# Half of the adjacency factors made on VectorE in the first group of heads, with two side queues that start late

## The chip, the cores and the metric

The kernel runs on one core of one Trainium2 chip. The metric is the device time in microseconds of one launch, taken as the median of several runs.

## The reference, cut to what matters

Two layers of a graph network are computed for 3327 nodes with 128 features, over one adjacency matrix `adj` of zeros and ones. The first layer is a graph attention layer, the second has 128 attention heads of width 8 (d is the number of heads here, h the width).

```python
# layer 0
H = X @ W.T + b
e = leaky_relu(A * (H @ a_s) + A * (H @ a_r).T, 0.2)
att = softmax(where(A > 0, e, NEG), axis=1)
x = layernorm(x + att @ H)
# layer 1: q, k, v are (d, n, h) with d = 128 heads of width h = 8
a = einsum('dnh,dmh->dnm', q, k) * d ** -0.5
a = softmax(a + adj + adj, axis=2)          # both encodings are adj
out = einsum('dnm,dmh->dnh', a, v).reshape(n, h * d)
x = layernorm(x + out @ Wo.T)
```

The second layer costs nearly all of the time: 128 heads with a score matrix of 3327 x 3327 each.

## The kernel before, in words

**Groups, blocks, rounds.** The heads are taken in NG = 32 groups of HG = 4. A group takes the queries in NBLK = 7 blocks of 476 (the last has 472). A block goes over NT = 26 tiles of up to 128 keys in NR = 26 rounds, so a group has `total` = 182 rounds. In each round, TensorE makes two halves of scores (two heads of one key tile each, 128 x 952), and TensorE multiplies an earlier key tile's weights by the values, LAG = 5 rounds behind (line 957). The exponential is exp(2(s + adj)), since scores are scaled by one half of the usual factor.

**Two ways to put adj in.** Key tiles are taken in threes (a *stretch*, three rounds; a block has nine stretches or, in the other order, ten). Two tiles of a three are *added*: VectorE writes scores + adj (line 1177), and ScalarE takes the exponential of all four heads at once (line 1000, 128 x 1904). The third is *multiplied*: ScalarE takes the exponential of the bare scores (line 1174, 128 x 952), and GpSimd multiplies it by a factor, 1 where adj is 0 and e squared where it is 1 (line 1175). So a block has 17 or 18 multiplications on GpSimd and 34 or 35 additions on VectorE.

**The factors.** Each block of queries has nine factor tiles of 128 x 476. They are made once, in the first group of heads, by `make_factor` (line 794): one multiply-and-add in place, at the end of the stretch ahead of the one that uses it. Two rounds later SyncE stores it to device memory (`ftd`), from where every later group loads it. That makes 63 factors, all in group 0. Loads of adj are issued AHEAD = 3 stretches in advance from SyncE's queue (`want_adj`).

**The side work.** Layer 0 for row tile 0 is done before the groups begin. Row tiles 1 to 25 of layer 0, with their projections to q, k and v, and the final projection of each tile (`result`) are spread between the rounds. `work` and `work_tensor` take units from three queues, in this order: `main` (products, normalization, projections, results), `aside` (weights of a tile: `weigh` line 308 and `mask` line 317, both on GpSimd, kind "m") and `counts` (`count`, line 326 on VectorE, kind "d"; it counts zeros and ones of adj for a check, and after each six counts the queue loads a part of the next tile's adj). `lane` gives one place for a "d" unit and one for an "m" unit about every third round, 7 of each in a block; the first queue that has a unit of the kind at its head takes the place. A unit "n" at the head of a queue waits for a mark, "t" sets one, "w" waits some rounds. A tile is worked on in three chunks of 9, 9 and 8 key tiles.

**Due times.** `finish_to` at round 164 of a group runs at once whatever the next group still needs: tile 1 for group 1, tile 2 for group 2, and so on.

The order on each engine is fixed when the program is built. The few lines that set the places:

```python
n -= odd
if n == NR - 2 and odd:
    return int(kind != "l")
if kind == "l" and n == -1:
    return 1
if n < 6:
    return int(kind == "l" and n == 0 and not odd)
return int(n % 3 == {"q": 0, "l": 2}.get(kind, 1) or n % 3 == 1 and kind == "q")
```

Of the kernel before, what the change touches and what calls it, by code (L numbers as in the profile page):

```python
# [13 lines left out]
ALU = mybir.AluOpType  # L14
# [13 lines left out]
E2 = 7.38905609893065  # L28
# [19 lines left out]
def kernel(  # L48
# [27 lines left out]
    nc = tc.nc  # L76
# [73 lines left out]
    def special():  # L150
# [9 lines left out]
        with ExitStack() as sx, tc.manual_schedule(engines=ALL):  # L160
# [94 lines left out]
            def issue(f):  # L255
                pend.append([ISSUE, f])
# [485 lines left out]
            def kind(g, b):  # L742

                return (g * NBLK + b) % 2
# [41 lines left out]
            def make_factor(n):  # L786
                if n < len(stretches):
                    g, b, m = stretches[n]
                    times, _ = plans[kind(g, b)][m]
                    if times is None or made_by[b, times] != n:  # L790
                        return
                    w = exact[b][2]
                    f = adjs[n][:, 0, :w]
                    nc.gpsimd.tensor_scalar(f, f, E2 - 1.0, 1.0, op0=ALU.mult, op1=ALU.add)  # L794
                    issue(lambda: nc.sync.dma_start(ftd[b][times // 3][:, :w], f))


# [209 lines left out]
            total = NBLK * NR  # L1007
# [19 lines left out]
            made = [layer0(t) for t in range(1, NT)]  # L1027
            first_loads = made[0][0]
            main = []
            aside, counts = [], []  # L1030
            for n, (_, m, a) in enumerate(made):

                k = 0
                for u in a:
                    if u[0] == "r":

                        at = max((k for k, v in enumerate(aside) if v[0] == "n" and v[1][0] == "P"), default=0)
                        aside.insert(at, ("x", u[1]))
                    elif isinstance(u, list):
                        counts += u  # L1040
                        if n + 1 < len(made):
                            counts += [("n", ("W", (n + 1) * len(CH) + k, 0)), made[n + 1][0][k], ("t", ("L", (n + 2) * len(CH) + k))]
                        k += 1
                    else:
                        aside.append(u)
                main.append(m)
# [8 lines left out]
            def head(row, now, force=False):  # L1055

                while True:
                    if not side[row]:
                        if row != "main":
                            return None  # L1060
                        ahead = ("rows", reads[min(max(now, 0) // total + 2, NG - 1)]) in marks
                        if results and results[0][0] <= now and (ahead or not main):
                            side[row] = results.pop(0)[1]
                        elif main:
                            side[row] = main.pop(0)
                        else:
                            return None
                    kind, f = side[row][0]
                    if kind == "t":
                        marks[f] = now  # L1070
                    elif kind == "w":
                        if not force and now - side["since"][row] < f:
                            return None
                    elif kind == "n":
                        if f[:2] not in marks or not force and now - marks[f[:2]] < f[2]:
                            return None
                    else:
                        return kind
                    side[row].pop(0)
# [5 lines left out]
            def work_tensor(now, n, odd):  # L1085

                kind = head("main", now)
                if kind in ("p", "q") and lane(kind, n, odd) and side["read"] != now - 1:
                    run("main", now)

            def work(now, n, odd):
                room, low, pool = lane("d", n, odd), lane("l", n, odd), lane("m", n, odd)
                for row in ("main", "aside", "counts"):
                    while True:
                        kind = head(row, now)
                        if kind == "x":
                            pass
                        elif kind == "d" and room:
                            room -= 1
                            if row == "main":  # L1100
                                side["read"] = now
                        elif kind == "l" and low:
                            low -= 1
                            side["read"] = now
                        elif kind == "m" and pool:
                            pool -= 1
                        else:
                            break
                        run(row, now)

            def finish_to(mark, now):
                while mark not in marks:
                    at = -1 if now is None else now
                    row = next((row for row in ("main", "aside", "counts") if head(row, at, True)), None)
                    if row is None:
                        break
                    run(row, -1)
                    tick(True)
# [9 lines left out]
            for _, u in first_loads:  # L1128
                u()
            nc.sync.dma_start(wo, woT)  # L1130
            make_factor(0)
            for g in range(NG):
                k4, v4, _ = group
                for b in range(NBLK):
# [5 lines left out]
                    for n, rnd in enumerate(rounds):  # L1140
                        at = b * NR + n
                        if n in starts:
                            m = number[g, b, starts[n]]
                            want_adj(m + AHEAD)
                            a = adjs[m]
# [33 lines left out]
                        now = g * total + at  # L1179
# [4 lines left out]
                        if n + 1 in starts or n + 1 == NR:  # L1184
                            del adjs[m]
                            make_factor(m + 1)
# [139 lines left out]
    def general():  # L1326
        with ExitStack() as gx:
# [168 lines left out]
            with ExitStack() as pc:  # L1496
                wp = pc.enter_context(tc.tile_pool(name="pc_w", bufs=3))
                ps = pc.enter_context(tc.tile_pool(name="pc_ps", bufs=4, space=bass.MemoryType.PSUM))
                for t in range(NT):
# [30 lines left out]
                    nc.scalar.dma_start(out[t * P : t * P + r, :], y[:r])  # L1530

    special()
    fine = nc.values_load(flag[0:1, 0:1])
    with tc.If(fine < 1):
# [41 lines left out]
```

## Time and profile before

| what | us |
|---|---|
| median of 3 runs (lowest to highest) | 9987.08 (9984.36 to 9990.81) |
| the profiled execution's own time | 9985.2 |
| its span, first to last instruction | 9983.4 |
| ScalarE busy in it | 9866.4 (99%) |
| TensorE, VectorE, GpSimd busy | 9441.9, 9189.1, 9175.6 |
| a block of queries at about 645 us | 44.0 |
| a block of queries at about 150 us | 51.7 |

Block times are read from the timeline of VectorE: line 967 copies the finished block once (124.30, 175.98, 227.56, 278.74, 329.34, 373.98, 423.47, 467.14, 512.83 us and so on), so the distance of two copies is one block. Group 0 holds the first seven copies.

### The profile page before, as it was taken

To read this page: it belongs to the slowest core of one execution; us is meant where nothing else is said; L and a number is where in the kernel's file an instruction comes from. 1 tells how busy PE (TensorE), PEld (TensorE's weight loads), DVE (VectorE), ACT (ScalarE), POOL (GpSimd) and SP (SyncE) were. 2 spreads that over 40 slices of the span, in tenths; PEclk is the share of its full clock that TensorE was granted. 3 is DMA by queue.
4 is the path that set the end of the run, shared out by engine and by line. 5 is a ranking of instruction groups with operands and counts; after the bars stand their busy time and mean duration, and the time that the engine had idled before them with its cause. 6 is when DMAs were issued, how large, how long until landed. Compare 5 with 4: busy or idle time off the path is not lost.

```text
span 9983.4 us, 207568 instructions
## 1 busy us (share of the span) xinstructions
PE 9441.9 (95%) x79523; PEld 2997.2 (30%) x79523; DVE 9189.1 (92%) x10554; ACT 9866.4 (99%) x7904; POOL 9175.6 (92%) x4954
## 2 busy tenths in 40 slices
PE   7999999999999999999999999999999999999998
PEld 2233233333332333323333233233333322222222
DVE  7899999999999999999999999999999998888888
ACT  7999999999999999999999999999999999999999
POOL 7999899999999999999999999999999988888887
PEclk8999999999999999999999999999999999999999
DMA  6666665666656566565566665666665655555554
GB/s 195 201 185 182 176 185 170 180 182 178 183 172 185 164 182 191 169 187 172 169 183 183 188 175 171 180 180 176 186 169 176 176 164 166 163 158 168 165 166 133
DMA packets 1399415, 1755.28 MB, mean 176 GB/s; under 512 B 349361, under 2 KB 1386891, under 8 KB 1394313
## 3 DMA queue, kind: packets, MB, share of 16 engines
q1 hardware_dynamic: 1388061, 1739.30, 60.5%
q8 instruction: 626, 10.26, 0.4%
q10 hardware_dynamic: 10347, 2.61, 0.1%
q14 instruction: 381, 3.11, 0.1%
HBM read 1637.49 MB, written 103.93 MB: 174 GB/s over the span
## 4 chain that ended last, share of the span: by engine, by line
ACT 43%; PE 30%; issue 10%; POOL 10%; DVE 5%; DMA 1%; SPq 0%; POOLq 0%; DVEq 0%; ACTq 0%
ACT e L1000 31%; PE av L957 15%; PE scb L152 12%; ACT e L1174 12%; POOL e L1175 9%; DVE e L1177 4%; PE bank L241 2%; DVE o L967 1%; DMA at<-in_adjT_dram 1%; POOL w L308 0%; POOL w L317 0%; POOL at L794 0%; DVE lo L409 0%; DMA at<-ftd 0%; DVE dump L326 0%
## 5 line engine op out<-in xcount | busy, mean ns | idle before, releaser
L1175 POOL TENSOR_TENSOR e<-e,at 128x952 f32<-128x952 f32 (+1 forms) x3920 | 8715.4, 2238 | 720.0 <-ACT e L1174 673.0
L1177 DVE TENSOR_TENSOR e<-scb,at 128x952 f32<-128x952 f32 (+1 forms) x7728 | 8501.1, 1142 | 724.3 <-PE scb L152 518.9
L1000 ACT ACTIVATE e<-e 128x1904 f32<-128x1904 f32 (+3 forms) x3920 | 7488.3, 1910 | 10.4 <-DVE e L1177 8.8
L957 PE MATMUL av<-e,v4b 128*32 128x476 f32 (+1 forms) x46592 | 5815.9, 573 | 77.8 <-DVE o L967 36.8
L1174 ACT ACTIVATE e<-scb 128x952 f32<-128x952 f32 (+1 forms) x3920 | 4314.7, 1101 | 53.3 <-PE scb L152 25.2
L152 PE MATMUL scb<-q4b,k4b 32*128 32x476 f32 (+1 forms) x23296 | 3854.1, 485 | 430.1 <-ACT e L1174 302.3
L152 PEld LDWEIGHTS scb<-q4b,k4b 32*128 32x128 f32 (+1 forms) x23296 | 1746.4, 189 | 5403.3 <-ACT e L1174 3189.4
L957 PEld LDWEIGHTS av<-e,v4b 128*32 128x32 f32 (+1 forms) x46592 | 1030.0, 108 | 1244.3 <-issue 1011.5
L241 PE MATMUL bank<-hsb,w 128*32 128x129 f32 (+1 forms) x5200 | 278.3, 286 | 0.0
L326 DVE TENSOR_SCALAR_CACHE_REDUCE dump<-a 128x384 bf16<-128x384 f32 (+2 forms) x468 | 247.3, 528 | 0.6
L308 POOL TENSOR_SCALAR w<-trow,er 128x129 f32<-128x129 f32 x650 | 233.2, 383 | 1.9
L317 POOL TENSOR_TENSOR w<-w,a 128x384 f32<-128x384 f32 (+3 forms) x225 | 209.5, 931 | 0.1
L967 DVE COPY o<-av 128x476 f32<-128x476 f32 (+1 forms) x224 | 144.1, 643 | 7.4 <-PE av L957 7.3
L241 PEld LDWEIGHTS bank<-hsb,w 128*32 128x32 f32 (+1 forms) x5200 | 102.5, 108 | 148.1 <-issue 148.1
L241 PE MATMUL bank<-wo,ot 128*32 128x128 f32 x1600 | 85.2, 285 | 0.0
L402 DVE TENSOR_SCALAR hi<-bank 128x256 fp32r<-128x256 f32 (+1 forms) x200 | 82.8, 414 | 0.0
L409 DVE SCALAR_TENSOR_TENSOR lo<-bank,hi 128x256 fp32r<-128x256 f32 (+1 forms) x200 | 82.8, 414 | 0.0
L241 PE MATMUL bank<-wk,x1T 128*32 128x256 f32 x800 | 63.9, 391 | 0.0
L241 PE MATMUL bank<-wq,x1T 128*32 128x256 f32 x800 | 63.9, 391 | 0.0
L241 PE MATMUL bank<-wv,x1T 128*32 128x256 f32 x800 | 63.9, 391 | 0.0
L503 PE MATMUL bank<-ident,o 128*128 128x128 f32 x225 | 52.0, 304 | 0.0
L290 POOL MEMSET a<- 128x128 f32 (+1 forms) x25 | 5.2, 208 | 45.8 <-DVE dump L326 44.9
(123 smaller groups left out, 653.2 us busy)
## 6 DMA issues: line engine op xcount, KB each, us to landing
at<-in_adjT_dram SPq DMA_DIRECT2D x1536, 476.0 KB
at<-ftd SPq DMA_DIRECT2D x1674, 238.0 KB
at<-in_adjT_dram SPq DMA_DIRECT2D x256, 472.0 KB
at<-ftd SPq DMA_DIRECT2D x279, 236.0 KB
k4b<-kT SPq DMA_DIRECT2D x128, 415.9 KB
q4b<-qT SPq DMA_DIRECT2D x1528, 29.8 KB
at<-in_adjT_dram SPq DMA_DIRECT2D x192, 208.2 KB
at<-in_adjT_dram SPq DMA_DIRECT2D x150, 238.0 KB
```

The costliest lines, as they stand in the source:

```text
L152: nc.tensor.matmul(dst, k4[32 * j : 32 * j + H4, first_key(i) : first_key(i) + 2 * r - 1 : 2], q4[32 * j : 32 * j + H4, :nb], start=True, ...
L241: nc.tensor.matmul(dst[c0:c1], w[:, c0:c1], mov, **kw)
L308: nc.gpsimd.tensor_scalar(w, s["t"][:, :, :T3], -LOWEST, e, op0=ALU.min, op1=ALU.max)
L317: nc.gpsimd.tensor_tensor(w, w, s["a"][n][:, c0 - i0 : c1 - i0, :r], op=ALU.mult)
L326: nc.vector.tensor_scalar(z, a, float(k), None, op0=ALU.is_equal, op1=ALU.add, accum_out=even[:, t, at : at + 1])
L402: nc.vector.tensor_scalar(hi[:r, o : o + QW], s["b"][:r, :QW], scale, None, op0=ALU.mult)
L957: nc.tensor.matmul(s.av[32 * j : 32 * j + 32, : s.w], s.v4[:r, j, i * H1 : i * H1 + 32], e[:r, j, : s.w], start=(s.left == NT - 1), stop=( ...
L967: nc.vector.tensor_copy(o4[:, :w], s.av[:, :w])
L1000: nc.scalar.activation(e, e, AF.Exp, scale=2.0)
L1174: nc.scalar.activation(eh, z[:r, :, :w], AF.Exp, scale=2.0)
L1175: nc.gpsimd.tensor_tensor(eh, eh, ah, op=ALU.mult)
L1177: nc.vector.tensor_tensor(eh, z[:r, :, :w], ah, op=ALU.add)
```

## The change

1. `make_factor` takes VectorE for the stretches of odd number in a block and keeps GpSimd for the others. With nine factors in a block, VectorE gets four in blocks 0, 2, 4 and 6 of group 0 and five in blocks 1, 3 and 5: 31 of 63.
2. A new kind of unit, "a", holds its queue until a given round. The queue `counts` begins with one for round `total * 3 // 5` = 109.
3. The queue `aside` gets one for round `total * 4 // 5` = 145 ahead of the weights of row tile 2 (the second tile of this queue).

```diff
-                    nc.gpsimd.tensor_scalar(f, f, E2 - 1.0, 1.0, op0=ALU.mult, op1=ALU.add)
+                    engine = nc.vector if m % 2 else nc.gpsimd
+                    engine.tensor_scalar(f, f, E2 - 1.0, 1.0, op0=ALU.mult, op1=ALU.add)
                     issue(lambda: nc.sync.dma_start(ftd[b][times // 3][:, :w], f))
...
-            aside, counts = [], []
+            aside, counts = [], [("a", total * 3 // 5)]
             for n, (_, m, a) in enumerate(made):
 
                 k = 0
+                if n == 1:
+                    aside.append(("a", total * 4 // 5))
                 for u in a:
...
+                    elif kind == "a":
+                        if not force and now < f:
+                            return None
                     elif kind == "n":
```

## The prediction

> **What bounds the kernel now.** I read the page first (busy time, costliest groups), then the stretches of time cut at the block copies of line 967, then who waits for whom in group 0.
>
> ```profile
> PE 9441.9 (95%) x79523; PEld 2997.2 (30%) x79523; DVE 9189.1 (92%) x10554; ACT 9866.4 (99%) x7904; POOL 9175.6 (92%) x4954
> L1175 POOL TENSOR_TENSOR e<-e,at 128x952 f32<-128x952 f32 (+1 forms) x3920 | 8715.4, 2238 | 720.0 <-ACT e L1174 673.0
> L1177 DVE TENSOR_TENSOR e<-scb,at 128x952 f32<-128x952 f32 (+1 forms) x7728 | 8501.1, 1142 | 724.3 <-PE scb L152 518.9
> L1000 ACT ACTIVATE e<-e 128x1904 f32<-128x1904 f32 (+3 forms) x3920 | 7488.3, 1910 | 10.4 <-DVE e L1177 8.8
> ```
>
> ScalarE bounds the kernel as a whole: 99% busy, 10 us idle before line 1000. But that is an average, so I cut it by blocks (columns: length; PE, PEld, DVE, ACT, POOL busy; granted clock; DMA share; GB/s).
>
> ```profile
> 72.00:124.30 52.30, 44.38 (x330) 13.21 (x328) 43.75 (x52) 50.06 (x40) 49.74 (x42) 0.92 0.68 201
> 124.30:176.00 51.70, 46.67 (x392) 14.87 (x392) 41.10 (x51) 43.66 (x35) 49.86 (x40) 0.87 0.66 198
> 176.00:227.60 51.60, 43.41 (x404) 14.23 (x404) 42.19 (x51) 46.69 (x35) 49.79 (x40) 0.99 0.62 184
> 227.60:278.70 51.10, 45.83 (x348) 13.15 (x348) 41.74 (x55) 44.34 (x35) 49.17 (x40) 0.91 0.61 187
> 278.70:329.30 50.60, 44.00 (x365) 13.22 (x365) 42.81 (x49) 45.16 (x36) 48.97 (x36) 0.97 0.64 190
> 329.30:374.00 44.70, 42.44 (x370) 13.16 (x370) 40.91 (x46) 44.50 (x36) 43.19 (x27) 1.00 0.83 249
> 374.00:423.50 49.50, 45.13 (x428) 15.10 (x426) 41.92 (x52) 46.31 (x36) 47.95 (x36) 0.97 0.89 229
> 645.00:689.00 44.00, 42.57 (x404) 14.63 (x402) 41.78 (x53) 44.00 (x36) 44.00 (x31) 1.00 0.54 157
> ```
>
> The last row is a usual block: ScalarE 44.00 of 44.0. In group 0 six blocks of seven are 5 to 8 us longer, ScalarE has gaps, and GpSimd is busy all but 2 us, which are the small gaps around its 36 to 42 instructions. **Group 0 is GpSimd's.** The waits between 120 and 450 us say the same; in a usual group TensorE waits for ScalarE instead.
>
> ```profile
> PEld av L957 <- POOL e L1175: 41.5, 44, 3.2
> PE av L957 <- POOL e L1175: 28.3, 33, 2.9
> ```
>
> The seven blocks take 350.9 us (423.5 - 72.6), and 7 x 44 = 308: at most **43 us (0.43%)** can be won. Nothing else in the span is short of ScalarE.
>
> **What the Trainium skill says.** (1) "SBUF — State Buffer", section "Who interferes with whom": VectorE and GpSimd share one pair of ports. A tensor_scalar on VectorE in a 2-port mode takes it as an exclusive lock; who starts first keeps it for the whole instruction and the other blocks. The form that also writes its accumulator is excepted. The trace has no plain tensor_scalar of any size from SBUF to SBUF beside GpSimd, so it shows no such block. It agrees on the exceptions: the counts (accumulator form) and the additions (one SBUF input) keep their length under a busy GpSimd.
>
> ```profile
> L794 POOL TENSOR_SCALAR at<-at x63: 584/588/592, 56.3 to 417.3; 128x476 f32<-128x476 f32 x54, 128x472 f32<-128x472 f32 x9
> L326 DVE TENSOR_SCALAR_CACHE_REDUCE dump<-a x468: 407/543/553, 45.5 to 7744.6; 128x384 bf16<-128x384 f32 x125, 128x256 bf16<-128x256 f32 x25, 128x381 bf16<-128x381 f32 x5, 128x254 bf16<-128x254 f32 x1
> L1177 DVE TENSOR_TENSOR e<-scb,at x7728: 1084/1141/1152, 66.8 to 9955.1; 128x952 f32<-128x952 f32 x164, 128x944 f32<-128x944 f32 x27, 127x952 f32<-127x952 f32 x7, 127x944 f32<-127x944 f32 x1
> ```
>
> (2) "VectorE: DVE Perf Modes", section "The perf-mode tier table": fp32 tensor_scalar from SBUF runs at two elements a cycle. No run here shows it.
>
> **Prices.** GpSimd, start to start: multiplication 2.21 (4.42 for two in the timeline), factor 0.65 (0.59 and its gaps), weigh 1.08, mask 0.98. VectorE: addition 1.09 (3.26 for three), block copy 0.65, count 0.63, hi or lo 0.41. The factor on VectorE: by the skill's page (2), section on the TRN2 errata, its measured fixed term of 150 cycles and 476/2 at 0.96 GHz give an estimate of 0.40 us; with the 58 cycles of its table 0.31; the copy of 476 columns at line 967 took 0.64, the upper end. I take 0.40. The wait for the port is unknown: from 0 to what is left of a multiplication, 1.1 us on average, 2.2 at most.
>
> **The change, part by part.**
>
> *Where the side units land.* "m" and "d" places are rounds 7, 10, ... 25 of an even block and 8, 11, ... 23, 25 of an odd one. Tile 1 is not touched: its 18 weigh and mask units and one bias fill 7, 7 and 5 places of blocks 0 to 2, and its chain on VectorE runs from round 89 to 153, as the trace has it. In the kernel before, tile 2 follows at once: 2, 7, 3, 0 and 4 units in blocks 2 to 6. After it, the counts may go from round 109, but `main` holds every "d" place up to 153: first count at 155, the sixth at 175, and only then is tile 2's first chunk loaded. So the weights start at 178, and the wait to 145 decides nothing. Group 0 keeps 7, 7, 5, 0, 0, 0, 2 units of 35; 14 units leave it. The three loads move to rounds 175, 199 and 221 of SyncE's queue; before, block 6 had two loads of the next tile (rounds 163 and 181), so its DMA share (0.89) does not grow by them.
>
> *Sum by block* (us). GpSimd before = 18 or 17 multiplications + 9 x 0.65 + units; after, 4 or 5 factors cost it only 0.40, while VectorE holds the port. VectorE after = 35 or 34 additions + copy + main and counts + 4 or 5 factors of 0.40, with 0.3 of wait in blocks 3 to 6.
>
> | block | GpSimd before | GpSimd after | VectorE after | after |
> |---|---|---|---|---|
> | 0 | 52.8 | 51.9 | 40.4 | 51.9 |
> | 1 | 50.6 | 49.4 | 39.6 | 49.4 |
> | 2 | 52.0 | 49.0 | 40.4 | 49.0 |
> | 3 | 50.9 | 42.2 | 43.9 | 44.0 |
> | 4 | 48.6 | 44.7 | 47.3 | 47.3 |
> | 5 | 43.4 | 42.2 | 45.1 | 45.1 |
> | 6 | 49.7 | 46.8 | 45.9 | 46.8 |
>
> Before, with 44 for block 5, this makes 348.6 against 350.9 measured, so the sum can be trusted to some 3 us. After: 333.5, **15 less**. Of that about 14 come from the units (removed from a queue that is the bound), and little from the factors: under the lock GpSimd saves 0.25 each, and in block 4, where VectorE has seven hi/lo pairs, VectorE becomes the bound (38.7 + 5.8 + 2.8).
>
> Why 0.3 of wait where GpSimd is not behind: in the timeline at 565 us VectorE ends a stretch's additions at 565.1, GpSimd's multiplication ends at 565.31, and the next starts at 565.61. The factor falls into that gap. In blocks 0 to 2 GpSimd has no gap, but there VectorE has 9 to 11 us to spare: four or five waits of 1.1 are hidden; without that cover they are rival 2.
>
> *Given back.* Tile 2 puts 7, 7, 7, 2 units into blocks 7 to 10 (in need 178 us of GpSimd, against 177.6 measured before). I take 1 us. The counts left out of blocks 0 to 3 (22) fill empty places later; blocks near 9000 us, with no side work, are 43.8 to 44.05 long like the others, so moving it costs nothing. By the places, tile 2 ends at round 331; it is due at 346. If it were late, the rest would run at once, some 5 us.
>
> *On the queues.* SyncE stores a factor two rounds after it is issued; a VectorE factor is done by then, and loads are three stretches ahead, so nothing behind it is late. Behind a waiting factor on VectorE stand lo and the next additions; ScalarE waits for these.
>
> Sum: -15 + 1 = -14. Against the profiled 9985.2 that is 9971; the median stands 1.9 higher, so **9973**, within 0.2% of before.
>
> **The rivals.**
>
> *1. The port costs nothing visible.* Then GpSimd saves the whole 0.65 for 31 factors: blocks 50.2, 47.4, 47.3, 44, 46, 44.5, 45.1, together 324.5, and -23 with the 1 given back: **9964**. For it: each engine's small gaps could let the other in. Against it: the skill's lock.
>
> *2. The wait for the port is on the chain; slower.* The units alone give -14. If a factor on VectorE holds up its additions, the scores' buffers stay full, TensorE stops in its order, and ScalarE with it. If c is what each of the 31 factors adds to the chain, the sum is -14 + 31c: no gain from c = 0.45. With half a multiplication (1.1) and 0.15 of the factor itself, c = 1.25 and the sum is +25: **10012**. For it: GpSimd's multiplications follow each other without a gap in blocks 0 to 2 (4.42 for two), so VectorE may get the port only when GpSimd runs dry, and VectorE has but a us or two of slack in blocks 4 to 6. Against it: the gap at 565.31, and 9 to 11 us of slack in blocks 0 to 2.
>
> *3. Half of the change does nothing:* as worked out, the wait to round 145 decides nothing. That is in the forecast.
>
> **How the numbers follow.** Forecast 0.42, its own range -25 to -4 (the factor at 0.31 to 0.64, the wait at 0 to 1.1 in blocks 4 and 5, the sum's own 3 us): 0.12 of it faster by over 0.2% (20 us, about what a measurement of this kernel can tell from no change), 0.30 within. Rival 1 0.35, range -32 to -16: 0.28 faster, 0.07 within. Rival 2 0.23, range 0 to +50: 0.15 slower, 0.08 within. Sum: faster 0.40, within 0.45, slower 0.15. The range 9955 to 10000 leaves out 0.03 of rival 1 and 0.15 of rival 2.
>
> **What would show it.** Blocks 0 to 2 at about 50 with GpSimd busy, 3 to 6 at 44 to 47, from block 7 on 44. No weights between rounds 70 and 178 on GpSimd, no counts before 155. Factors on VectorE of 0.4 us where GpSimd pauses and 1 to 2.5 us where it does not: the lock. All at one length: rival 1. Blocks 4 to 6 no shorter than before, with ScalarE waiting for line 1177: rival 2. A longer block anywhere after group 0 would make the whole reading wrong.

## The result and the profile after

The changed kernel takes 9969.69 us (18 runs, 9965.05 to 9977.7) against 9986.88 us before (18 runs, 9983.58 to 9991.83): a ratio of 0.9982, 95% interval 0.9975 to 0.9989, so 17 us less. 9973 was forecast, with a range of 9955 to 10000. The profiled execution took 9966.7 us, its span 9964.9. Where one profile is compared with another below, each is counted from its own first exponential of group 0 (67.87 us before, 66.22 in the changed kernel), since that start differs by some us from one profile to the next. Counted so, group 0 ends 355.6 us after its start before and 338.2 now, 17.4 us less: all of the gain.

Group 0 by blocks, cut at the copies of the finished blocks (now line 968). This view of the changed kernel has the columns of the one before: length; PE, PEld, DVE, ACT, POOL busy; granted clock; DMA share; GB/s.

```profile
72.00:125.30 53.30, 48.25 (x328) 12.83 (x324) 44.25 (x42) 46.96 (x37) 50.19 (x39) 0.83 0.71 220
125.30:173.80 48.50, 44.81 (x394) 14.47 (x394) 43.88 (x40) 45.67 (x36) 46.68 (x34) 0.93 0.60 185
173.80:221.80 48.00, 43.73 (x402) 14.34 (x402) 43.72 (x42) 44.16 (x35) 46.43 (x32) 0.96 0.60 180
221.80:267.40 45.60, 42.51 (x346) 13.04 (x346) 44.32 (x59) 45.10 (x36) 42.28 (x23) 1.00 0.70 215
267.40:313.70 46.30, 44.22 (x363) 13.51 (x363) 44.32 (x55) 44.20 (x35) 41.24 (x24) 0.96 0.69 209
313.70:359.40 45.70, 42.69 (x362) 13.08 (x362) 44.23 (x51) 44.90 (x36) 42.00 (x22) 1.00 0.75 226
359.40:404.40 45.00, 42.11 (x314) 12.13 (x314) 43.27 (x54) 43.36 (x35) 41.21 (x27) 0.96 0.94 254
404.40:448.30 43.90, 41.40 (x346) 13.15 (x346) 40.70 (x51) 43.90 (x36) 43.80 (x33) 1.00 0.59 183
645.00:689.00 44.00, 43.03 (x416) 14.76 (x416) 41.28 (x47) 44.00 (x36) 42.46 (x25) 1.00 0.74 194
```

Blocks 1 to 4 and 6 are 3 to 5.5 us shorter than before, block 5 is 1 us longer, and the blocks from 404 to 1400 us have the old 43.5 to 44.2. From block 1 on, GpSimd's busy time is 1 to 8 us lower in each block of group 0, and VectorE's rises to 43 to 44. Block 0 is no shorter: its copy comes 59.1 us after the first exponential, 56.4 before, and TensorE's granted clock (the share of full speed that it was given) fell there from 0.92 to 0.83. That wasn't forecast.

The line of the factors, one row for each engine (duration in ns: shortest, median, longest):

```profile
L795 POOL TENSOR_SCALAR at<-at x32: 584/588/591, 54.8 to 395.1; 128x476 f32<-128x476 f32 x27, 128x472 f32<-128x472 f32 x5
L795 DVE TENSOR_SCALAR at<-at x31: 398/719/2275, 70.6 to 388.3; 128x476 f32<-128x476 f32 x27, 128x472 f32<-128x472 f32 x4
```

GpSimd's factors all have one length. VectorE's begin at 0.398 us, the estimate of 0.40, and go up to 2.275: the wait is inside the recorded duration. Wherever one waited for long, it ends 0.26 to 0.27 us after the GpSimd instruction in front of it. In the waits of the changed kernel between 120 and 450 us, GpSimd no longer stands among the first; ScalarE and VectorE do.

```profile
PEld scb L152 <- ACT e L1180: 79.8, 90, 1.5
PEld scb L152 <- DVE e L1183: 52.3, 77, 1.9
...
PE scb L152 <- DVE e L1183: 14.4, 30, 1.0
```

### The profile page after: what moved, and what is told of

The parts are those of the page before. It is cut to its first block, busy times and chain, and to the rows that moved or that the text cites. A ratio compares the mean times of both kernels' runs of the same rounds, so it can differ in the third digit from the quotient of the medians.

```text
span 9964.9 us, 207575 instructions
## 1 busy us (share of the span) xinstructions
PE 9447.6 (95%) x79523; PEld 3001.4 (30%) x79523; DVE 9208.5 (92%) x10585; ACT 9859.0 (99%) x7904; POOL 9158.4 (92%) x4923
## 4 chain that ended last, share of the span: by engine, by line
ACT 42%; PE 33%; issue 9%; POOL 7%; DVE 5%; DMA 1%; SPq 0%; POOLq 0%; DVEq 0%; ACTq 0%
ACT e L1001 30%; PE av L958 17%; PE scb L152 14%; ACT e L1180 12%; POOL e L1181 7%; DVE e L1183 4%; PE bank L241 3%; DVE o L968 1%; DMA at<-in_adjT_dram 0%; POOL w L308 0%; POOL w L317 0%; DVE dump L326 0%; DVE lo L409 0%; PE bank L503 0%; DVE x1T L509 0%
## 5 line engine op out<-in xcount | busy, mean ns | idle before, releaser
L290 POOL MEMSET a<- 128x128 f32 (+1 forms) x25 | 5.2, 208 | 43.9 <-DVE dump L326 43.0
```

## The experiments

The questions: what of the 17 us is the side units' and what the factors', whether the waits for the port cost time, and whether anything is left. "Theory" is the prediction's; its rivals are 1 (the port costs nothing) and 2 (the wait is on the chain).

### The two waits alone

```diff
-                    engine = nc.vector if m % 2 else nc.gpsimd
+                    engine = nc.gpsimd
```

> The two waits are kept, all 63 factors are made on GpSimd again. Theory of the prediction (14 us come from side units that leave group 0, the factors on VectorE bring next to nothing): 14 us faster than before, about 9973, with blocks 0 and 1 at 51.7 as before, block 2 at 50, blocks 3 and 5 at 44, block 4 at 45.6, block 6 at 47.7. Rival 1 (the port costs nothing and the factors bring some 9 us): only 8 us of the 17 are left, about 9979. Rival 2 (the waits for the port are on the chain): faster than the changed kernel, 22 us or more under before, about 9965.

Measured: 9973.47 us against 9984.59, ratio 0.9989 (0.9982 to 0.9996), 11 us less. Blocks 1 to 6 take 52.1, 51.2, 44.7, 46.5, 44.7 and 47.4 us. So the waits bring about two thirds, near the theory's 14; block 8, with seven units, takes 46.9, and there some is given back. Of the changed kernel's gain some 6 us are missing here. The two intervals overlap, but the profiles agree: the ninth copy comes 432.5 us after the first exponential, in the changed kernel 426.1. So VectorE's factors bring more than the theory's 1, less than rival 1's 9, and rival 2 (faster than the changed kernel) falls.

### The second wait alone, moved to round 176, counts free

```diff
-            aside, counts = [], [("a", total * 3 // 5)]
+            aside, counts = [], []
...
-                    aside.append(("a", total * 4 // 5))
+                    aside.append(("a", 176))
...
-                    engine = nc.vector if m % 2 else nc.gpsimd
+                    engine = nc.gpsimd
```

> All factors on GpSimd, no wait for the counts, and the weights of tile 2 wait until round 176. So GpSimd has the units of the run with both waits alone (which was 11 us faster than before), at the same rounds, but the counts stay on VectorE in blocks 0 to 2 as before. If the gain of the waits is the GpSimd work that leaves group 0: the same 11 us, about 9974. If it is the counts that no longer stand ahead of VectorE's additions: a third of it or less, about 9981.

Measured: 9978.12 us against 9987.35, ratio 0.9990 (0.9984 to 0.9997), 9 us less: the same as with both waits, within the intervals. What the waits bring is GpSimd's work that leaves group 0; whether the counts stay on VectorE hardly matters. The wait to round 145 as the change has it decides nothing: by the length of block 5 that round is at about 340 us (an estimate), and the first weights of tile 2 start at 393.97 us in the changed kernel.

### The factors on VectorE alone

```diff
-            aside, counts = [], [("a", total * 3 // 5)]
+            aside, counts = [], []
...
-                if n == 1:
-                    aside.append(("a", total * 4 // 5))
```

> The factors of the odd stretches on VectorE as in the change, neither of the two waits. Theory of the prediction: about 3 us faster than before (0.25 us of GpSimd for each of the 31 factors, less what their waits cost), about 9984. Rival 1: 9 us faster, about 9978, and no factor on VectorE longer than 0.5 us. Rival 2: 10 us or more slower than before, since counts and factors now both stand ahead of the additions in blocks 0 to 2.

Measured: 9975.69 us against 9984.59, ratio 0.9991 (0.9983 to 0.9999), 9 us less. The two parts alone make 11 + 9 = 20, the whole 17: they add up within the intervals. The gain has rival 1's size, but not its mechanism; the factors on VectorE are not of one length:

```profile
L795 DVE TENSOR_SCALAR at<-at x31: 396/1025/2285, 69.5 to 395.3; 128x476 f32<-128x476 f32 x27, 128x472 f32<-128x472 f32 x4
```

### All 63 factors on VectorE

```diff
-                    engine = nc.vector if m % 2 else nc.gpsimd
+                    engine = nc.vector
```

> Both waits as in the change, but all 63 factors on VectorE. This doubles the disputed cost. Theory of the prediction: VectorE becomes the bound from block 3 on (38.7 of additions and copy, 9 factors of 0.7, 5.8 of projections in block 4, so 50.8 there), and the whole is some 10 us slower than the changed kernel, about 9980. Rival 1: GpSimd saves 0.65 for 32 more factors, blocks 0 to 2 lose 3 us each, about 9960. Rival 2 with c = 1.25 for each of 63 factors against -14: +65, about 10050.

Measured: 9968.81 us against 9984.59, ratio 0.9984 (0.9978 to 0.9991), 16 us less, no different from the changed kernel. All three expectations miss: VectorE as the bound from block 3 on, 0.65 us saved for each factor, and rival 2's 1.25 us lost for each. Block 4 took 46.2 us, not 50.8, and the median of all 63 factors was 0.565 us (shortest 0.390, longest 2.397). Why the median is lower than with 31 is open; GpSimd, with less to do, may pause more. The second half of the factors neither gained nor lost.

### The same factors in a form that doesn't take the shared port

```diff
-                    engine = nc.vector if m % 2 else nc.gpsimd
-                    engine.tensor_scalar(f, f, E2 - 1.0, 1.0, op0=ALU.mult, op1=ALU.add)
+                    if m % 2:
+                        nc.vector.tensor_scalar(
+                            f, f, E2 - 1.0, None, op0=ALU.mult, op1=ALU.add, accum_out=fsum[:, 0:1]
+                        )
+                    else:
+                        nc.gpsimd.tensor_scalar(f, f, E2 - 1.0, 1.0, op0=ALU.mult, op1=ALU.add)
```

> As the changed kernel, but the 31 factors on VectorE are made by the form of the instruction that also writes its accumulator, as the counts are; that form leaves out the addition of 1, so the values of these factors are not those of the reference. From the counts of 384 columns (0.54 and 0.08 for the accumulator) it takes about 0.64 + 0.08 = 0.72 us for 476 columns, and by the skill it doesn't use the port that GpSimd shares. If the waits for the port (31 factors took 32.3 us in the changed kernel, 19.9 of it over 0.40 each) cost time on the chain: all 31 at 0.64, blocks 0 to 2 at 1 to 3 us less, 5 us faster than the changed kernel in all, about 9965. If the waits are hidden: no faster than the changed kernel, 9970 or, since 0.72 in blocks 4 and 5 is as long as 0.40 with its wait there, the same there too.

Measured: 9957.12 us (9952.57 to 9962.64) against 9984.59, ratio 0.9973 (0.9963 to 0.9983): 27 us less than before, and 10 us more gained than by the changed kernel, whose runs it doesn't overlap. In the profiles group 0 ends 327.5 us after its first exponential, 10.8 earlier than in the changed kernel. Its factors:

```profile
L796 DVE TENSOR_SCALAR_CACHE_REDUCE at<-at x31: 633/639/640, 70.0 to 377.1; 128x476 f32<-128x476 f32 x27, 128x472 f32<-128x472 f32 x4
L796 DVE DVE_READ_ACCUMULATOR at<-at x31: 81/83/85, 70.5 to 377.6; 128x1 f32 x31
```

An instruction that is 1.6 times as long as the other one's shortest, but always the same, makes the kernel faster. All 31, with their accumulator reads, take 31 x 0.72 = 22.4 us, the plain ones of the changed kernel 32.3. **The waits for the port cost time on the chain, about 10 us in all.** A place is in the timeline of the changed kernel (start, duration, engine, line, names):

```profile
90.63 4.41 POOL L1181 TENSOR_TENSOR e<-e,at 128x952 f32<-128x952 f32 x2
...
93.28 2.03 DVE L795 TENSOR_SCALAR at<-at 128x476 f32<-128x476 f32 x1
...
95.23 3.25 DVE L1183 TENSOR_TENSOR e<-scb,at 128x952 f32<-128x952 f32 x3
...
96.42 0.48 PE L152 MATMUL scb<-q4b,k4b 32*128 32x476 f32 x2 [0.73 <-DVE e L1183]
...
97.51 1.79 ACT L1001 ACTIVATE e<-e 128x1904 f32<-128x1904 f32 x1 [0.77 <-DVE e L1183]
```

VectorE issues the factor at 93.28, while GpSimd is in the second of two multiplications that ends at 95.04. It gets the port then, ends at 95.31, and the additions behind it start 1.6 us later than behind a factor of 0.40. TensorE waits 0.73 us for a score buffer and ScalarE 0.77 for its input. The same place with the accumulator form, which runs beside the second multiplication:

```profile
89.78 4.42 POOL L1186 TENSOR_TENSOR e<-e,at 128x952 f32<-128x952 f32 x2
...
92.76 0.64 DVE L796 TENSOR_SCALAR_CACHE_REDUCE at<-at 128x476 f32<-128x476 f32 x1
...
93.32 2.20 DVE L1188 TENSOR_TENSOR e<-scb,at 128x952 f32<-128x952 f32 x2
...
96.10 1.81 ACT L1006 ACTIVATE e<-e 128x1904 f32<-128x1904 f32 x1
```

The profiles speak against two other explanations. GpSimd could be what the plain factors hold up; but its 20th multiplication starts 55.6 us after the first exponential in the changed kernel and 55.2 here, while the copy of block 0 comes 59.1 and 53.5 us after it. And the values differ here, since a factor is 0 where adj is 0; but the run below with the same split, the accumulator form and the right values (scaled values) has that copy at 54.8, although its GpSimd has more to do.

### ScalarE for the early factors

```diff
+                    if m % 2 and b < 3:
+                        nc.scalar.activation(f, f, AF.Exp, scale=2.0)
+                    else:
+                        engine = nc.vector if m % 2 else nc.gpsimd
```

> As the changed kernel, but in blocks 0 to 2 the 13 factors of odd stretches are made by ScalarE (exp of 2 adj, which is 1 or e squared) instead of VectorE. If the waits for the port in blocks 0 to 2 are what the accumulator form won (10 us): some 8 us faster than the changed kernel, about 9960 to 9962, since ScalarE has 3 to 6 us of idle time in these blocks and a factor costs it about 0.5. If ScalarE has no room there: no faster than the changed kernel, 9968 or more.

Measured: 9968.63 us against 9987.35, ratio 0.9981 (0.9973 to 0.9989), 19 us less: within the intervals no better than the changed kernel. Block 1 falls to 46.3, but block 2 takes 50.3 and block 3, where VectorE's plain factors begin again (longest 2.42 us), 48.4. At the end of block 2 the run is 4.0 us ahead of the changed kernel, and it loses 2.8 of that in block 3. To see if that was the port:

```diff
-                        engine = nc.vector if m % 2 else nc.gpsimd
+                        engine = nc.gpsimd
```

> As the run with ScalarE in blocks 0 to 2, but from block 3 on GpSimd makes all factors, so that no factor takes the port on VectorE. That run lost its gain of 3 us at the end of block 1 again in blocks 2 and 3. If that was by factors on VectorE waiting for the port at the start of block 3 (one took 2.4 us): about 5 us faster than that run, 9963, block 3 at 44 to 45. If it was ScalarE, late by its own factors in blocks 0 to 2: the same as that run or slower, 9968 to 9973, since GpSimd now has 13 to 14 more factors in blocks 4 and 6.

Measured: 9966.39 us against 9984.05, ratio 0.9982 (0.9975 to 0.9989), 18 us less. Block 3 is 44.3, as expected without the port; but blocks 6 and 8 are 47.3 and 46.5, where GpSimd has the factors and then tile 2's units. The gain of block 3 went there.

### A form with nothing left out

```diff
+                            f, f, 1.0 / (E2 - 1.0), None, op0=ALU.add, op1=ALU.add, accum_out=fsum[:, 0:1]
...
+                        nc.gpsimd.tensor_scalar(f, f, 1.0 / (E2 - 1.0), None, op0=ALU.add)
...
-                                nc.scalar.activation(eh, z[:r, :, :w], AF.Exp, scale=2.0)
+                                nc.scalar.activation(eh, z[:r, :, :w], AF.Exp, scale=2.0, bias=lnf[:r])
```

> The accumulator form with nothing left out: all 63 factors are adj + 1/(e^2 - 1), one operation (31 on VectorE in the accumulator form, 32 on GpSimd), and the missing scale e^2 - 1 goes into the bias of the exponential that they multiply. If a bias costs ScalarE nothing: as the accumulator form before, 27 us faster than the kernel before, about 9957. If it costs 10 ns in each of the 3920 exponentials, about 9996.

> As the version with the sum in the accumulator form, but in blocks 0 to 2 VectorE makes all nine factors. GpSimd has 44 to 47 us of work there then, VectorE 44 to 45. If GpSimd is still the bound in these blocks: 1 us less in block 0 and 2 to 3 us less in blocks 1 and 2, 5 us faster than that version, about 9952. If VectorE's place in the order is the bound there already: no faster, 9957 or more.

Measured: 10300.06 us against 9987.35, ratio 1.0314 (1.0300 to 1.0328), and with all nine factors of blocks 0 to 2 on VectorE (`if m % 2 or b < 3`) 10291.67, ratio 1.0304 (1.0290 to 1.0318). Both are slower by over 300 us: the bias isn't free. The exponential of bare scores, first with the bias, then in the changed kernel without:

```profile
L1187 ACT ACTIVATE e<-scb,lnf x3920: 1032/1293/1464, 65.5 to 10278.7; 128x952 f32<-128x952 f32 x168, 128x944 f32<-128x944 f32 x28
```
```profile
L1180 ACT ACTIVATE e<-scb x3920: 939/1097/1287, 66.2 to 9936.6; 128x952 f32<-128x952 f32 x168, 128x944 f32<-128x944 f32 x28
```

313 us over 3920 exponentials is 80 ns each, on the engine that bounds the kernel. (The recorded median grows by more, 196 ns, and that of the exponentials without a bias on ScalarE's other line grows too, from 1925 to 2031 ns, so recorded lengths overstate it.) So the scale was put elsewhere, into the values of the nine multiplied tiles:

```diff
+                        if at == 3:
+                            v = v4[:, :, : NT * H1].rearrange("p j (i e) -> p j i e", e=H1)[:, :, 0:NT:3, :]
+                            nc.gpsimd.tensor_scalar(v, v, E2 - 1.0, None, op0=ALU.mult)
```

> The sum in the accumulator form again (31 factors on VectorE, 32 on GpSimd, as in the changed kernel), but without the bias: the missing scale is put into the values of the nine multiplied key tiles, by one GpSimd instruction of 324 elements in round 3 of each group. If the 313 us of the version with the bias were the bias alone: 25 to 28 us faster than before, about 9961, the same as the first accumulator form, since the 32 new instructions (some 0.5 us each) fall on GpSimd where it has 5 us of slack in a block. If it was the sum or the new form: slower than before.

> As the version with scaled values, but VectorE makes all nine factors in blocks 0 to 2. With the bias this brought 8 us (10300 to 10292). If the gain is GpSimd's in blocks 0 to 2: 5 to 8 us faster than the version with scaled values, about 9954, blocks 1 and 2 at 45 to 46. If with the bias it only hid behind the slower ScalarE: no difference.

Measured: 9982.38 us against 9984.05, ratio 0.9998 (0.9990 to 1.0007), no gain left; and with VectorE making all factors of blocks 0 to 2, 9963.61, ratio 0.9980 (0.9973 to 0.9987). The bias was indeed the 313 us, but the first is 25 us slower than the accumulator form with its addition left out. The trace shows one reason; GpSimd's factors, with one operation, are not 0.59 us long:

```profile
L800 POOL TENSOR_SCALAR at<-at x32: 1390/1402/1434, 52.5 to 394.8; 128x476 f32<-128x476 f32 x27, 128x472 f32<-128x472 f32 x5
```

That is 32 x 0.81 us = 26 us more on GpSimd, in the group that it bounds; but group 0 is only 11.9 us longer than with the accumulator form. Another 9.1 us are lost after it, where the 32 scales, 1.07 us each, are new: TensorE's products wait for them 11 times, 11.8 us in all. But TensorE was at half clock for 29 us of that time, 20 with the accumulator form, so how much of the 9.1 is the scales' is open. With an idle second operation:

```diff
-                        nc.gpsimd.tensor_scalar(f, f, 1.0 / (E2 - 1.0), None, op0=ALU.add)
+                        nc.gpsimd.tensor_scalar(f, f, 1.0, 1.0 / (E2 - 1.0), op0=ALU.mult, op1=ALU.add)
...
-                            nc.gpsimd.tensor_scalar(v, v, E2 - 1.0, None, op0=ALU.mult)
+                            nc.gpsimd.tensor_scalar(v, v, E2 - 1.0, 0.0, op0=ALU.mult, op1=ALU.add)
```

> As the version with scaled values in which VectorE makes all factors of blocks 0 to 2, but GpSimd's two one-operation instructions get a second, idle one (times 1 ahead of the sum, plus 0 behind the scale). With one operation a GpSimd factor took 1.40 us in the trace, with two 0.59 in the kernel before, for the same 476 columns; 18 of them are on GpSimd, and 32 scales took 1.07 us each. If that length is of the form with one operation: both fall to about 0.59 and 0.45, block 7 (47.2) goes to 44 to 45, and the whole is 5 to 8 us faster, about 9957. If GpSimd hides them anyway: no difference, 9964.

Measured: **9955.64 us** against 9988.84, ratio 0.9967 (0.9955 to 0.9980), 33 us less than before: the lowest median of this study, with nothing left out.

```profile
L800 POOL TENSOR_SCALAR at<-at x18: 587/590/593, 208.0 to 376.5; 128x476 f32<-128x476 f32 x13, 128x472 f32<-128x472 f32 x5
```

Blocks 1 to 7 take 43.9, 44.0, 44.3, 45.4, 44.5, 44.0 and 43.8 us: but for block 4, ScalarE's pace. The 32 scales now take 0.48 us each; what they still cost is not shown. With the plain form, giving VectorE all 63 factors had brought nothing (above); in the accumulator form, giving it all of blocks 0 to 2 brings these blocks to ScalarE's pace.

## Why the prediction was right

**The bound.** Right. Group 0 was GpSimd's, and all of the gain lies there (355.6 to 338.2 us).

**Where the units land.** Right to the block: the first count of the side queue is in block 5 (350.65 us), tile 2's first weights in block 6 (393.97 us), long after the wait to round 145 had ended.

**The units' 14 us.** Right in size: 11 us, or 9 with the counts left free.

**Price of the factor on VectorE.** 0.40 forecast, 0.398 the shortest. The estimate from the Trainium skill's "VectorE: DVE Perf Modes", section on the TRN2 errata, agrees with this trace, with the measured fixed term of 150 cycles (0.40 us) and not the table's 58 (0.31).

**The lock.** Right. The Trainium skill's "SBUF — State Buffer", section "Who interferes with whom", is what the trace shows: plain factors wait (0.398 to 2.275 us), the accumulator form does not (0.633 to 0.640).

**The waits.** Forecast 1.1 on average in blocks 0 to 2 and 0.3 in blocks 3 to 6. The first 13 factors on VectorE average 1.37 us, so 0.97 of wait, the last 18 average 0.81, so 0.41. Both sizes are right.

**The cover in blocks 0 to 2.** This step failed in block 0. VectorE's 9 to 11 us to spare were to hide its waits. Against the accumulator form, counted from the first exponential, the changed kernel loses 5.5 us in block 0, 0.6 in blocks 1 and 2 together, and 4.6 in blocks 3 to 6, where the forecast had priced a wait. So in blocks 1 and 2 the cover held. In block 0 the lag of ScalarE can be followed exponential by exponential (lines 1001 and 1006): none up to 94 us, 0.8 us behind the factor of 93.28, 2.7 at 104 us, 3.4 ahead of the factor of 117.19 and 5.3 behind it. With the waits alone, and with the scaled values, there is no such lag up to that place. VectorE's idle time in a block was no cover there, since the additions behind the factor feed ScalarE at once through a few score buffers.

Some 2 of these 5 us fall into a stretch with TensorE at half clock (0.50 granted from 97.5 to 104.1 us, TensorE busy all of it; eight value products take 1.82 us there, 1.01 before and after). Whether the waits brought it on is not shown. With all 63 factors on VectorE the clock is full from 83 us to the end of block 0, and block 0 is still 3.7 us longer than with the accumulator form, though VectorE has more factors there than in the changed kernel. So rival 2's mechanism is at work, with a price far under the 1.25 a factor that it named: 10/31 = 0.3.

**GpSimd's saving.** Mis-sized where it counts. The forecast took 0.25 a factor, on the view that GpSimd stands still for 0.40 while VectorE holds the port. That is what the trace shows where a multiplication follows: GpSimd pauses 0.40 us ahead of it. But 17 of these 20 pauses lie from block 3 on, where GpSimd is no longer the bound; up to the end of block 2 only 3 of 14 factors are followed by one. In half of the 14 cases a unit of weights comes next, and GpSimd starts it 0.10 us after the multiplication, as it also does with the accumulator form. Against the waits alone, GpSimd's 53rd multiplication, the last of block 2, comes 7.0 us sooner after the first exponential, 0.53 for each of 13 factors. This miss and that of the cover have opposite signs and offset each other.

**The factors' gain.** Forecast at about 1 us; 6 measured as the difference of the whole and the waits alone, 9 alone. In the profiles the changed kernel is ahead of the waits alone by 2.6 us at the end of block 2, 3.2 at the end of group 0 and 6.4 two blocks later. That last part was not in the forecast: with the waits alone tile 2's units make block 8 46.9 us long, in the changed kernel it is 44.0.

**Block by block.** 51.9, 49.4, 49.0, 44.0, 47.3, 45.1, 46.8 forecast; 54.3, 48.5, 48.0, 45.6, 46.2, 45.8, 45.0 measured. (Block 0 is counted from 70.95 us, since the group began 1.65 us earlier than in the profile before; from the prediction's 72.6 it is 52.7.) Both sums are 333.5: the total is better than its parts, and that is luck, since misses of -1.8 to +2.4 us cancel. The 1 us given back later wasn't: blocks 7 and 8 took 43.8 and 44.0 against 43.7 and 45.7 before.

## What to carry to other kernels

Cut the trace into stages first: an engine with 92% of the whole span bounded one group of 32, and work that wasn't due in that group could be moved later at little cost (11 us won). An instruction moved from GpSimd to VectorE has to be priced with its wait for the shared port (up to 2.3 us here), not by its own length alone (0.40), and a form that stays off the port can win although it is longer. Idle time of an engine covers a wait only if what is queued behind the waiting instruction isn't needed before the idle time comes.

## What the runs showed that was not expected

- A tensor_scalar on GpSimd with one operation takes 1.40 us for 128 x 476 fp32, and 0.59 us with two.
- A bias taken from a tile costs about 80 ns in each exponential of 128 x 952, by the kernel's time: 313 us over 3920 against the kernel before, 314 against the run with the same factors and no bias (each taken from its own kernel before).
- VectorE got the port at the end of the multiplication that was running, never after two: the longest of the 31 factors was 2.275 us, the longest in any run 2.42, and a multiplication takes 2.24, with 0.27 from its end to the factor's.
- ScalarE makes a factor of 476 columns in 0.64 us (median of 13), and the kernel gained nothing by it, though ScalarE had 3 to 6 us of idle time in those blocks.
